# Attention and convolution-row matmuls in 64x64 tiles, row weights loaded pair by pair, and separate tiles for the second projection's weights and tokens

## The chip, the cores and the metric

The kernel runs on one core of one Trainium2 chip. Its time is the device time of one execution in microseconds; "before" is the median of three executions. The engines are called as the profile calls them: PE (TensorE matmul), PEld (its weight loads), DVE (VectorE), ACT (ScalarE), POOL (GpSimd) and SP (SyncE, which here does nothing but issue DMAs).

## The reference

Two layers work on x of shape (4, 512, 128, 64), in float32. B is 4, T is 512, and a token has D = 128 x 64 = 8192 channels.

```python
# layer 0, x as (b, t, d)
xn = layernorm(x);  k, v = xn @ Wk, xn @ Wv;  r = sigmoid(xn @ Wr)      # d -> 64
s_t = decay * s_(t-1) + k_t * v_t                                       # scan over t
x = x + (r * states) @ Wo                                               # 64 -> d: "attend"
x = x + gelu(conv3(layernorm(x)) + freq_b)                              # 64 -> 64 channels, along f
x = x + layernorm(depthwise_causal_conv3(layernorm(x)) + time_b)        # along t
x = x + gelu(x @ W1 + b1) @ W2 + b2                                     # 64 -> 256 -> 64
# layer 1
trend = moving_average(x, 25);  xf = rfft(x - trend)[:128 modes]
x = trend + irfft(xf mixed by complex weights of each channel)
```

## The kernel before

Layer 0 holds a batch's x with channels on the 128 partitions: 64 chunks of 128 channels by 512 tokens, taken as NPR = 32 pairs of chunks. For each batch b these stages run, named by letters in the code:

- J `project`: k, v and r for all pairs, accumulated in one PSUM pair of banks (L414). Each pair needs its projection weights, x with channels on partitions (`xp`, 512 KB), and x with tokens on partitions (512 KB), of which DVE takes the layernorm statistics (`bn_stats`, L346). The first batch also accumulates sums of the weights (L406).
- Z `scan`: a serial chain of small steps on PE, DVE, ACT and POOL that ends in `rst`, the gated states, and in the mean and deviation of the next layernorm.
- A `attend_and_convolve`: step i does `attend(i)`, `convolve(i - 2)` and the sums of pair i - 3 (`add_up`, L253). `attend` loads `xp` (L296) and `wo_sb` (L532), multiplies (L536), and DVE adds xp (L538) and scales (L542). `convolve` writes one pair of PSUM banks in three groups: the rows (L557: a product over two rows that carries the layernorm's mean and the constant term, four matmuls), the neighbours (L566: the convolution's reach across the chunks' edges, four 64x64 matmuls) and the chunk itself (L571: two 128x128 matmuls). ACT applies gelu (L572), DVE adds (L574), POOL's queue stores, ACT squares (L579).
- C `convolve_time`, O `open_feed`, F `feed_forward` (L743 widens and L758 narrows, both in 64x64 tiles; L779 transposes back to tokens).

"64x64 tiles" means that a matmul uses a quarter of PE's array: the partitions of its operands select the row half, the partitions of its output the column half, and four of them can run side by side. Before, attention uses two tiles of 64 rows by 128 columns, and the rows use four of 32 rows by 64 columns, for which `cgr` keeps the rows' weights of all 32 pairs at partitions 0, 32, 64 and 96. They are loaded once, by four DMAs on ACT's queue (L212).

PE's order is written out by hand (`manual_schedule`). `in_turn` runs two streams side by side and picks at each yield the one that is behind:

```python
((0, (Z, 0.12), (A, 0.88)), (1, (J, 0.88), (Z, 0.12))),      # A0 beside J1
((0, (C, 1.0)), (1, (A, 1.0))),                              # C0 beside A1
((0, (O, 0.05), (F, 0.95)), (2, (J, 0.88), (Z, 0.12))),      # F0 beside J2
((1, (C, 1.0)), (2, (A, 1.0))),                              # C1 beside A2
```

and so on. `project(0)` comes before all of it. On the other engines a scheduler orders the instructions when the program is built; each engine and each DMA queue then runs its list strictly in that order, and waits on semaphores.

Tiles come from pools with a fixed number of buffers. `fr` has the front stages' tiles (`xp`, `x1`, `z`, `wo`, `wcs`, `cgr`), `wxp` has two buffers of the tag `wx`. In J1, one `wx` buffer holds a pair's projection weights and its tokens together (L394), but for the first nine pairs, which borrow `x1` and `z`. In J2 and J3 a `wx` buffer holds the weights of two pairs (L354). In the last two feed-forwards it holds a pair of finished chunks (L766). Layer 1's pools `dft`, `slabs` and `io` reuse the storage from its start, in this order.

Of the kernel before, what the change touches and what calls it, by code (L numbers as in the profile page):

```python
# [10 lines left out]
F32 = mybir.dt.float32  # L11
# [5 lines left out]
P = 128  # L17
T = 512
NF = 128
H = 64  # L20
# [60 lines left out]
def layer0(ctx, tc, dram, x, xt, vecs, wkvr, wo, wdec, wconv, fbias, w1, fb1, w2, fb2, x4):  # L81
# [54 lines left out]
    fb2_sb = load("fb2_sb", fb2)  # L136


    sel = const.tile([P, 2, 2, S], F32, name="sel")
    for k in range(2):  # L140
        for i in range(2):
            nc.vector.tensor_copy(sel[:, k, i, :], ident[:, k * S : (k + 1) * S])
# [5 lines left out]
    nc.vector.tensor_copy(decb, dec.to_broadcast([P, T]))  # L148


    cgr = fr.tile([P, NPR, H], F32, name="cgr", bufs=1)

    at_one = const.tile([P, 2], F32, name="at_one")
    nc.vector.tensor_reduce(at_one[:, 0:1], ident.rearrange("p (q k) -> p q k", k=32)[:, :, 1], mybir.AxisListType.X, ALU.add)
# [15 lines left out]
    def prepare():  # L170
# [34 lines left out]
        nc.vector.tensor_copy(cgt, pg[:, 0, 0:P])  # L205
        for k in range(2):
            nc.scalar.dma_start(cgd[:, k, :], cgt[k * NCH : (k + 1) * NCH, :])
        cg4 = cgd.rearrange("(i j) k (h m) -> h j k i m", j=2, h=2)
        for h in range(2):
            for j in range(2):  # L210
                q = 32 * (2 * h + j)
                nc.scalar.dma_start(cgr[q : q + 2, :, :], cg4[h, j])  # L212

# [83 lines left out]
        return xp  # L297

    def spare(tag, n):
        if tag == "wx":  # L300
            return wxp.tile([P, 2, n], F32, tag=tag, name=tag)
        return fr.tile([P, 2, n], F32, tag=tag, name=tag, bufs=4 if tag == "z" else 3)

    def c_bank():
# [25 lines left out]
    def project(b):  # L330
# [20 lines left out]
        def weights(i):  # L351

            if i < NPR:
                w = spare("wx", 4 * S + SL).rearrange("p k n -> p (k n)")[:, 0 : 16 * S]  # L354
                w = w.rearrange("p (c s) -> p c s", c=4)
                nc.sync.dma_start(w, wkvr[2 * i : 2 * i + 4, :, 0 : 4 * S].rearrange("c p s -> p c s"))
                for k in range(2):
                    ws[i + k] = w[:, 2 * k : 2 * k + 2, :]
# [15 lines left out]
        for i in range(NPR):  # L374
            first, last = i == 0, i == NPR - 1
            if b > 1:


                xks[i] = token_major(i, two(bk, "sq" if i % 2 else "x2"))
                if i % 2 == 0:  # L380
                    weights(i + 2)
                if not last:
                    xps[i + 1] = load_x(b, i + 1)
                wq, xp = ws.pop(i), xps.pop(i)
                for k in (i - 2, NPR - 2, NPR - 1) if last else (i - 2,):
                    if k in xks:
                        statistics(k, xks.pop(k))
            else:
                if unscanned[0]:

                    wq, xk = two(fr, "x1")[:, :, 0 : 4 * S + 3], spare("z", SL)
                else:

                    both = spare("wx", 4 * S + SL)  # L394
                    wq, xk = both[:, :, 0 : 4 * S], both[:, :, 4 * S :]
                n = 4 * S + 2 * (b == 0)
                nc.sync.dma_start(wq[:, :, 0 : n], wkvr[2 * i : 2 * i + 2, :, 0 : n].rearrange("c p s -> p c s"))
                xp = load_x(b, i)
                statistics(i, token_major(i, xk))
            if b == 0:  # L400
                nc.gpsimd.memset(wq[:, :, n:], 1.0)
                for j in range(2):
# [24 lines left out]
    def scan(b):  # L427
# [43 lines left out]
        if b == 0:  # L471
            kv = two(fr, "x1")
        else:
            kv = spare("wx", 4 * S + SL)[:, :, 0:SL]
        for k in range(2):
            pk = bank()
            nc.tensor.matmul(
# [44 lines left out]
    def attend_and_convolve(b):  # L522
# [6 lines left out]
        def attend(i):  # L529
            xp = load_x(b, i)  # L530
            wo_sb = fr.tile([P, P], F32, tag="wo", name="wo_sb")
            nc.sync.dma_start(wo_sb, wo[:, i, :])  # L532
            at = two(ps_a, "a")
            for j in range(2):
                js = slice(j * S, (j + 1) * S)
                nc.tensor.matmul(at[:, j, :], lhsT=wo_sb[js, :], rhs=rst[js, :], start=True, stop=True)  # L536
            x1 = x1s[i] = fr.tile([P, 2, SL], F32, tag="x1", name="x1")
            nc.vector.tensor_tensor(x1, at, xp, ALU.add)  # L538
            z = fr.tile([P, 2, SL], F32, tag="z", name="z", bufs=4)
            for j in range(2):  # L540
                zs[2 * i + j] = z[:, j, :]
            nc.vector.tensor_tensor(z, x1, pair_of(rb), ALU.mult)  # L542

        def scaled(i):

            wcs = fr.tile([P, 2, P + H], F32, tag="wcs", name="wcs")
            for j in range(2):
                c = 2 * i + j
                ws[c] = wcs[:, j, :]
                nc.scalar.mul(wcs[:, j, :], wc_sb[:, i % 2, :], vec[:, G2, c : c + 1])  # L550

        def convolve(i):
            cv = c_bank() if i % 2 or held[0] else two(ps_m, "m")
            for h in range(2):
                for j in range(2):
                    q = 32 * (2 * h + j)
                    nc.tensor.matmul(  # L557
                        cv[h * H : (h + 1) * H, j, :], lhsT=cgr[q : q + 2, i, :], rhs=mb[q : q + 2, :],
                        start=True, stop=False,
                    )  # L560
            for j in range(2):
                c = 2 * i + j
# [162 lines left out]
    def feed_forward(b):  # L725
# [26 lines left out]
        def narrow(i, q):  # L752
# [10 lines left out]
                return  # L763
            x3 = x3s.pop(i)
            if lag > 1:
                pair = spare("wx", 4 * S + SL)[:, :, 0:SL]  # L766
# [130 lines left out]
def layer1(ctx, tc, x4, wri, dftv, dftd, dfte, idfte, idfto, avg, avgh, out, after):  # L897
# [67 lines left out]
    def transform(b, xf):  # L965

        for g in range(NS // 2):
            edge = slabs.tile([P, SL], F32, tag="edge", name="edge")
            uv, ev, pf = [], [], []
            for k in range(2):  # L970
                s = 2 * g + k
# [82 lines left out]
    def invert(b, xf):  # L1054
# [24 lines left out]
        def trends(s):  # L1079
            c = slice(s * SL, (s + 1) * SL)  # L1080
            xin = slab(b, s)
            halo = slabs.tile([P, SL], F32, tag="edge", name="halo")
            for j in range(NT):
                at = 32 * j
                if j > 0:
# [137 lines left out]
```

## Time and profile before

| | us |
|---|---|
| median of three executions (3697.53 to 3706.25) | 3703.95 |
| the profiled execution | 3708.95 |
| its span | 3707.2 |
| PE busy | 3520.8 (95%) |
| DVE busy | 2669.1 (72%) |
| ACT busy | 1778.5 (48%) |
| J0, then `scan(0)` | 0 to 166, to 225 |
| A0 beside J1 and its scan | 225 to 544 |
| C0 beside A1 | 544 to 815 |
| F0 beside J2 | 815 to 1205 |
| C1 beside A2 | 1205 to 1460 |
| F1 beside J3 | 1460 to 1862 |
| C2 beside A3 | 1862 to 2115 |
| F2 beside C3, then F3 | 2115 to 2480, to 2742 |
| layer 1 | 2742 to 3707 |

A line of the profile names the source line, the engine, the operation, the output and input tiles (buffer numbers left out), PE's tile shape where there is one, and the shapes; then how many, their busy time, and the mean duration of one in ns. A float32 matmul appears as two records, so x8 in the timeline are four matmuls. Times of the stages are read from the starts of their lines in the trace; neighbouring stages overlap a little.

### The profile page before, as it was taken

Reading aid. Unit: us, or ns where it says so; the run is one execution under the profiler, and the core shown is the slowest. Engines: PE = TensorE matmul, PEld = TensorE weight load, DVE = VectorE, ACT = ScalarE, POOL = GpSimd, SP = SyncE. Lnnn points to the kernel's source line nnn. Section 1 sums busy time; section 2 is a strip of 40 time slices with the busy share of each in tenths; the row PEclk is TensorE's granted clock in tenths of the full one; section 3 lists DMA queues with packets and bytes.
Section 4 is the critical chain, followed back from the end, with each engine's and each line's share of the span. In section 5 each row is a group of like instructions: output and inputs, shape, how many; then the busy total and the mean of one; then the engine's idle time right before and its main releaser. Section 6 shows DMA issues by size and latency. Waiting matters only on the chain. (4 is left out here: it accounts for less than half of the span.)

```text
span 3707.2 us, 52993 instructions
## 1 busy us (share of the span) xinstructions
PE 3520.8 (95%) x20041; PEld 1358.2 (37%) x20041; DVE 2669.1 (72%) x3498; ACT 1778.5 (48%) x2331; POOL 449.0 (12%) x654
## 2 busy tenths in 40 slices
PE   9999999989999999999999989999999999999998
PEld 4433322224433223433322333333333833328433
DVE  4445559986777896677789799956668277892677
ACT  0013336656666565666656588878864200152100
POOL 0000012220111121011112121100000000001000
PEclk9999989999999999999999999999999999999999
DMA  9857747777885687888568677746658478994687
GB/s 305 282 197 246 238 144 261 260 268 270 289 291 190 234 280 267 275 292 291 180 225 285 228 240 257 237 176 216 223 184 279 150 246 292 298 297 164 215 285 262
DMA packets 427223, 910.29 MB, mean 246 GB/s; under 512 B 32728, under 2 KB 83160, under 8 KB 422872
## 3 DMA queue, kind: packets, MB, share of 16 engines
q1 hardware_dynamic: 353136, 636.92, 52.6%
q0 software_dynamic: 71680, 268.46, 20.1%
q8 instruction: 160, 2.62, 0.3%
q10 hardware_dynamic: 2152, 1.51, 0.1%
q14 instruction: 95, 0.78, 0.1%
HBM read 638.26 MB, written 268.50 MB: 245 GB/s over the span
## 5 line engine op out<-in xcount | busy, mean ns | idle before, releaser
L758 PE MATMUL p<-mid,w_sb 64*64 64x512 f32 x2048 | 553.1, 597 | 17.5 <-DVE wx L771 17.5
L758 PE MATMUL pb<-mid,w_sb 64*64 64x512 f32 x2048 | 535.3, 597 | 0.0
L748 ACT ACTIVATE mid<-m,fb_sb 128x1024 f32<-128x1024 f32 x256 | 284.9, 1113 | 92.2 <-PE m L743 90.9
L748 ACT ACTIVATE mid<-c,fb_sb 128x1024 f32<-128x1024 f32 x256 | 284.5, 1111 | 92.2 <-PE c L743 90.0
L743 PE MATMUL c<-x,w_sb 64*64 64x512 f32 x2016 | 280.6, 609 | 13.9 <-ACT mid L748 7.6
L743 PE MATMUL m<-x,w_sb 64*64 64x512 f32 x2016 | 282.6, 612 | 7.4 <-ACT ob L792 5.3
L758 PEld LDWEIGHTS p<-mid,w_sb 64*64 64x64 f32 x2048 | 154.0, 135 | 292.4 <-issue 262.7
L1069 ACT COPY two<-a 128x512 f32<-128x512 f32 x64 | 37.5, 586 | 430.1 <-PE a L1064 430.1
L414 PE MATMUL a<-xp,wx 128*128 128x512 f32 x512 | 237.4, 608 | 0.5 <-DVE me L270 0.5
L1092 PE MATMUL b<-xin,avg_sb 128*128 128x512 f32 x512 | 230.8, 593 | 3.3 <-DVE xin L1098 3.3
L1098 DVE TENSOR_TENSOR xin<-b,pm 128x512 f32<-128x512 f32 x256 | 159.0, 683 | 98.7 <-PE b L1095 83.7
L579 ACT ACTIVATE sq<-x 128x1024 f32<-128x1024 f32 x128 | 135.1, 1055 | 184.0 <-DVE x L574 184.0
L634 DVE SCALAR_TENSOR_TENSOR to<-kd,vec,to 128x510 f32<-128x510 f32 (+1 forms) x272 | 196.8, 742 | 9.3 <-ACT to L630 8.2
L711 ACT ACTIVATE kd<-kd,vec 128x512 f32<-128x512 f32 x256 | 192.7, 803 | 3.3 <-DVE kd L703 3.3
L253 PE MATMUL st<-x,ones 128*32 128x512 f32 x512 | 175.6, 610 | 14.0 <-DVE x L574 14.0
L944 DVE COPY xf<-b 128x256 f32<-128x256 f32 x128 | 54.4, 425 | 178.9 <-PE b L1038 170.0
L714 DVE TENSOR_TENSOR x<-kd,kx 128x1024 f32<-128x1024 f32 x126 | 154.1, 1223 | 36.2 <-ACT kd L711 36.2
L634 DVE SCALAR_TENSOR_TENSOR z<-x,vec,z 128x511 f32<-128x511 f32 x240 | 175.8, 745 | 5.0 <-ACT z L630 3.6
L538 DVE TENSOR_TENSOR x<-a,xp 128x1024 f32<-128x1024 f32 x128 | 156.0, 1219 | 30.9 <-PE a L536 28.6
L536 PE MATMUL a<-rst,wo_sb 64*128 64x512 f32 x512 | 149.8, 659 | 26.2 <-DVE x L538 24.2
L577 POOL DMA_DIRECT2D x<-x x128 | 93.6, 731 | 569.7 <-DVE x L574 564.7
L771 DVE SCALAR_TENSOR_TENSOR x4t<-p,fb_sb,x 128x512 f32<-128x512 f32 x64 | 47.8, 746 | 159.5 <-PE pb L758 157.1
(269 smaller groups left out, 6823.4 us busy)
## 6 DMA issues: line engine op xcount, KB each, us to landing
xp<-in_xt SPq DMA_DIRECT2D x256, 512.0 KB
kh<-to SPq DMA_DIRECT2D x156, 512.0 KB
x<-x POOLq DMA_DIRECT2D x128, 512.0 KB, 4.6
kx<-x SPq DMA_DIRECT2D x128, 512.0 KB
x<-ob POOLq DMA_DIRECT2D x64, 1024.0 KB, 8.1
xin<-x SPq DMA_DIRECT2D x64, 1024.0 KB
out<-xin POOLq DMA_DIRECT2D x64, 1024.0 KB, 6.4
x<-x SPq DMA_DIRECT2D x96, 512.0 KB
```

The costliest lines, as they stand in the source:

```text
L253: nc.tensor.matmul(st[32 * q : 32 * q + 32, :], lhsT=ones, rhs=src[:, j, :], start=first, stop=last,)
L414: nc.tensor.matmul(pa[:, k, :], lhsT=wq[:, j, k * P : (k + 1) * P], rhs=xp[:, j, :], start=first and j == 0, stop=last and j == 1,)
L536: nc.tensor.matmul(at[:, j, :], lhsT=wo_sb[js, :], rhs=rst[js, :], start=True, stop=True)
L538: nc.vector.tensor_tensor(x1, at, xp, ALU.add)
L634: tap = nc.vector.scalar_tensor_tensor(to[:, j, k:], xr[:, j, : SL - k], vec[:, w, c], to[:, j, k:], ALU.mult, ALU.add)
L711: tc.keep_in_program_order(nc.scalar.activation(d[:, j, :], d[:, j, :], AF.Identity, bias=vec[:, B4, c], scale=vec[:, G4, c]))
L714: nc.vector.tensor_tensor(x3, d, x2, ALU.add)
L743: nc.tensor.matmul(pm[halves[j], h, :], lhsT=w1_sb[halves[h], q * H : (q + 1) * H], rhs=x3[halves[h], j, :], start=True, stop=True,)
L748: gelu = nc.scalar.activation(mid, pm, AF.Gelu_apprx_tanh, bias=fb1_sb[:, q : q + 1])
L758: nc.tensor.matmul(sums2[i][j][halves[h], :], lhsT=w2_sb[halves[j], q, :], rhs=mid[halves[j], h, :], start=q == 0, stop=q == 3,)
L1092: nc.tensor.matmul(po[j], lhsT=avg_sb[:, j, :], rhs=xin[:, j, :], start=True, stop=False)
L1098: nc.vector.tensor_tensor(by_n(xin[:, j, :]), by_n(po[j]), by_c(pm[j % 2][:, j // 2, :]), ALU.add)
```

## The change

- `attend` makes four matmuls of 64x64 out of two of 64x128.
- `convolve` makes the rows' matmuls over 64 partitions instead of two, in four 64x64 tiles. Their weights stand in three tiles `cg0`, `cg1` and `cg2` of 128x128 that are zero but for two rows in each half; `scaled(i)` loads these two rows for each chunk of pair i by two DMAs of 1 KB on SP's queue, into tile i % 3. `cgr` and its four DMAs go. (The rows of `mb` that meet zeros are any rows of it.)
- The neighbours' code is as it was.
- In J1, weights have a tag of their own, `wk` with two buffers, and tokens take `wx`, now 4 KB instead of 6 KB a partition, with three buffers. J1's statistics of a pair are written after the next pair's loads.
- The other users of `wx` have three buffers of it too. `sel` moves from `const` to `fr`; layer 1's `edge` and `halo` move from `slabs` to `io`, with as many buffers as before.

```diff
-    sel = const.tile([P, 2, 2, S], F32, name="sel")
+    sel = fr.tile([P, 2, 2, S], F32, name="sel", bufs=1)
...
-    cgr = fr.tile([P, NPR, H], F32, name="cgr", bufs=1)
+    cgs = [fr.tile([P, P], F32, name=f"cg{k}", bufs=1) for k in range(3)]
+    for cg in cgs:
+        nc.gpsimd.memset(cg, 0.0)
...
-        cg4 = cgd.rearrange("(i j) k (h m) -> h j k i m", j=2, h=2)
-        for h in range(2):
-            for j in range(2):
-                q = 32 * (2 * h + j)
-                nc.scalar.dma_start(cgr[q : q + 2, :, :], cg4[h, j])
...
-        if tag == "wx":
-            return wxp.tile([P, 2, n], F32, tag=tag, name=tag)
+        if tag in ("wk", "wx"):
+            return wxp.tile([P, 2, n], F32, tag=tag, name=tag, bufs=2 if tag == "wk" else 3)
...
-                    both = spare("wx", 4 * S + SL)
-                    wq, xk = both[:, :, 0 : 4 * S], both[:, :, 4 * S :]
+                    wq, xk = spare("wk", 4 * S), spare("wx", SL)
...
-                statistics(i, token_major(i, xk))
+                xks[i] = token_major(i, xk)
+                for k in (i - b, NPR - 1) if last else (i - b,):
+                    if k in xks:
+                        statistics(k, xks.pop(k))
...
             for j in range(2):
-                js = slice(j * S, (j + 1) * S)
-                nc.tensor.matmul(at[:, j, :], lhsT=wo_sb[js, :], rhs=rst[js, :], start=True, stop=True)
+                for hs in halves:
+                    nc.tensor.matmul(
+                        at[hs, j, :], lhsT=wo_sb[halves[j], hs], rhs=rst[halves[j], :], start=True, stop=True
+                    )
...
         def scaled(i):
+            for j in range(2):
+                at = H * (j ^ i % 2)
+                nc.sync.dma_start(cgs[i % 3][at : at + 2, :], cgd[2 * i + j])
...
-            for h in range(2):
-                for j in range(2):
-                    q = 32 * (2 * h + j)
+            for j in range(2):
+                rs = halves[j ^ i % 2]
+                for hs in halves:
                     nc.tensor.matmul(
-                        cv[h * H : (h + 1) * H, j, :], lhsT=cgr[q : q + 2, i, :], rhs=mb[q : q + 2, :],
-                        start=True, stop=False,
+                        cv[hs, j, :], lhsT=cgs[i % 3][rs, hs], rhs=mb[rs, :], start=True, stop=False
                     )
...
-            edge = slabs.tile([P, SL], F32, tag="edge", name="edge")
+            edge = io.tile([P, SL], F32, tag="edge", name="edge")
```

More of the change, by code (lines that the diff above doesn't have):

```diff
@@ L353, in weights @@
             if i < NPR:
-                w = spare("wx", 4 * S + SL).rearrange("p k n -> p (k n)")[:, 0 : 16 * S]
-                w = w.rearrange("p (c s) -> p c s", c=4)
+                w = spare("wx", SL).rearrange("p k n -> p (k n)").rearrange("p (c s) -> p c s", c=4)
                 nc.sync.dma_start(w, wkvr[2 * i : 2 * i + 4, :, 0 : 4 * S].rearrange("c p s -> p c s"))
@@ L473, in scan @@
         else:
-            kv = spare("wx", 4 * S + SL)[:, :, 0:SL]
+            kv = spare("wx", SL)
         for k in range(2):
@@ L765, in narrow @@
             if lag > 1:
-                pair = spare("wx", 4 * S + SL)[:, :, 0:SL]
+                pair = spare("wx", SL)
                 x4s[i] = [pair[:, j, :] for j in range(2)]
@@ L1081, in trends @@
             xin = slab(b, s)
-            halo = slabs.tile([P, SL], F32, tag="edge", name="halo")
+            halo = io.tile([P, SL], F32, tag="edge", name="halo")
             for j in range(NT):
```

## The prediction

> **What bounds the kernel now.** I read the page first, then busy time by stage, then the matmuls in order of time at one place of the attention stage and at one of the feed-forward, then the waits of the first attention stage. TensorE is the bound of the whole:
>
> ```profile
> span 3707.2 us, 52993 instructions
> ...
> PE 3520.8 (95%) x20041; PEld 1358.2 (37%) x20041; DVE 2669.1 (72%) x3498; ACT 1778.5 (48%) x2331; POOL 449.0 (12%) x654
> ...
> DVE  4445559986777896677789799956668277892677
> ```
>
> DVE reaches 9 in some slices, so stages must be told apart. These four stretches hold all of `attend_and_convolve`: A0 beside J1, A1 beside C0, A2 beside C1, A3 beside C2 (columns: length, then busy time of PE, PEld, DVE, ACT, POOL, granted clock, DMA share, GB/s). The last two rows cut the second stretch, and the chain that ends `scan(0)`.
>
> ```profile
> 225.00:544.00 319.00, 307.99 (x1335) 95.65 (x1335) 178.07 (x218) 104.42 (x146) 27.70 (x38) 0.97 0.66 220
> 544.00:815.00 271.00, 246.33 (x1231) 62.01 (x1233) 258.62 (x294) 160.93 (x219) 73.96 (x98) 0.98 0.76 261
> 1205.00:1460.00 255.00, 242.31 (x1372) 64.07 (x1364) 214.08 (x221) 152.66 (x207) 49.20 (x71) 0.99 0.75 256
> 1862.00:2115.00 253.00, 240.92 (x1324) 64.83 (x1320) 209.20 (x215) 146.30 (x197) 51.16 (x73) 0.97 0.73 249
> ...
> 700.00:750.00 50.00, 44.50 (x236) 10.53 (x228) 49.93 (x56) 31.48 (x43) 14.21 (x18) 1.00 0.76 256
> ...
> 186.00:228.00 42.00, 34.00 (x108) 16.18 (x108) 12.47 (x30) 5.63 (x7) 1.27 (x2) 0.96 0.35 117
> ```
>
> PE is busy 97%, 95% and 95% of stretches 1, 3 and 4. Stretch 2 belongs to DVE: 258.62 of 271, and in its middle 49.93 of 50. In `scan(0)` every queue has room.
>
> Now PE in order of time: first a pair of A1 (stretch 2), then the feed-forward, whose matmuls are 64x64 tiles already. The first column is the start; what a group costs is the distance to the next group's start, since ends overlap.
>
> ```profile
> 711.93 1.13 PE L536 MATMUL a<-rst,wo_sb 64*128 64x512 f32 x4
> 712.99 1.09 PE L557 MATMUL m<-rm,cgr 2*64 2x512 f32 x8
> 714.00 1.09 PE L566 MATMUL m<-z,wcs 64*64 64x512 f32 x8
> 715.02 1.98 PE L571 MATMUL m<-z,wcs 128*128 128x512 f32 x4
> ...
> 1005.64 1.09 PE L743 MATMUL m<-x,w_sb 64*64 64x512 f32 x8
> 1006.55 0.59 PE L758 MATMUL p<-mid,w_sb 64*64 64x512 f32 x2
> ...
> 1007.41 1.04 PE L743 MATMUL c<-x,w_sb 64*64 64x512 f32 x8
> ...
> 1011.70 0.59 PE L758 MATMUL p<-mid,w_sb 64*64 64x512 f32 x2
> ...
> 1012.67 0.70 PE L414 MATMUL a<-xp,wx 128*128 128x512 f32 x1
> ```
>
> A group of four 64x64 matmuls costs 0.86 (1006.55 to 1007.41) between neighbours of its own shape, 0.91 (1005.64 to 1006.55) just after another shape, 0.97 (1011.70 to 1012.67) just before another. Change of shape on both sides is then 0.86 + 0.05 + 0.11 = 1.02, which is what the rows (L557, 32x64 tiles: 1.01) and the neighbours (L566: 1.02) take. Attention (L536, two 64x128 tiles) takes 1.06.
>
> **The change part by part.**
>
> *Attention, rows and neighbours in one shape.* Where attention stands just before the rows, the three groups take 1.06 + 1.01 + 1.02 = 3.09 now; in one shape they take 0.91 + 0.86 + 0.97 = 2.74: 0.35 less. In the built order of PE, which the change does not alter otherwise, that is so for 106 of the 128 pairs (24, 26, 28 and 28 of the four batches). In the other 22, attention alone gains 1.06 - 1.02 = 0.04, rows with neighbours 2.03 - 1.88 = 0.15. Sum of PE: 106 x 0.35 + 22 x 0.19 = 41 us, some 10 to 10.6 in each stretch.
>
> Two rules of the Trainium skill bear on this. "TensorEngine Tiling (Array Packing)", Key Properties, says that a change of tiling mode drains the array; the trace puts 0.16 on each, which is the gain above. Its Gotcha 1 says that different row tiles cannot use one PSUM bank at a time. Today's rows write each bank from two row tiles, so by the rule they would run as two rounds, 2 x 0.86, and the new mapping (one row tile for each bank) would save another 0.86 x 128 = 110 us. The row is 1.01, one round; nothing is taken for it.
>
> What arrives on the end: stretch 1, PE-bound, all 10. Stretch 2: nothing, since PE only waits more for DVE, which has the same work. Stretches 3 and 4: PE idles some 12 of 255, of which about 7 for DVE (L538 and L574), and a faster PE meets DVE (84% busy) more often; I take 9 of 10.6 in each. Together 10 + 0 + 9 + 9 = 28.
>
> *Rows' weights loaded pair by pair.* Four early DMAs go from ACT's queue; 256 DMAs of 1 KB come onto SP's, two a pair, and three memsets on POOL before anything waits. "DMA: Bandwidth & Descriptors", Rules for kernel authors, speaks against this: under 64 KB one pays mostly overhead, with a fixed cost of about 2 us. Were it exposed, 256 x 2 = 512 us. The nearest rows are SP's issues of `wo_sb`, 0.42 to 0.53 us each. Two more make 0.9 us in a step of about 8.5 us (SP issues `xp` at 703.3 and 711.9), where SP now issues three and mostly waits. The wait that they add is for the rows three pairs earlier (L557); queued behind it on SP are `xp` and `wo_sb` of two pairs on. In the built order they stand between `wo_sb` and `xp` of pair i+2, and that `xp` waits for L538 of pair i-1 anyway, which falls in the step of that same L557. Landing has two steps, 17 us. So nothing, bounds 0 to 0.9 x 128 = 115 us if SP were the bound; nearest to 0, since no PE row waits for `xp` or `wo_sb` now.
>
> *J1's tokens and weights apart, statistics a pair later.* Now both share a buffer of two, so a token load waits for PE's matmuls. Apart, the tokens wait for DVE's statistics alone, and the built order pulls them far forward: 3 more of J1's token loads stand before J0's last pair on SP, and between DVE's first constants of `scan(0)` (186) and A0's first addition (L538, 228) come the statistics of 16 pairs, where none stood.
> - J0: 3 x 0.52 MB at its 300 GB/s is 5 us, if DMA is what ends it; 0, if PE is (busy 10.0 of 10 from 140 to 150). I take 3.
> - `scan(0)`: 16 pairs x 1.29 us of statistics = 21 us of DVE, which has 42 - 12.5 = 29 free; 8.4 MB beside the 4.9 moved there (117 GB/s x 42) is 13.3, at 300 GB/s 44 us of 42. Both just fit. But DVE takes them in order, and an instruction of the chain stands behind a statistic that waits for its landing or runs 0.65 us: I count some eight such places, 5 us. Bounds 0 and 53 (the third rival).
> - A0 beside J1: 19 statistics pairs and their waits leave DVE:
>
> ```profile
> DVE stt L346 <- DMA wx<-in_x: 40.5, 20, 4.2
> DVE wx L363 <- DMA wx<-in_wkvr: 40.0, 18, 4.5
> ```
>
> But PE, not DVE, is the bound there; of its 11 us idle only 3.9 are for L538. I take 1 of gain (0 to 4).
>
> *Storage.* `sel`, and `edge` and `halo` in another pool, cost no instruction. The first `edge` copies of layer 1 now stand behind the last copies of layer 0 on ACT (end 2743.1); three by 0.63 end at 2745, and PE takes them up at 2748.6. Third `wx` buffers in J2, J3 and the last feed-forwards: PE idles there for L771, not for a buffer. Nothing, 0 to 3 either way.
>
> Sum: -28 + 3 + 5 - 1 = -21 us. The profiled execution took 3708.95 (span 3707.2, 1.75 around it), 5.0 above the median of the runs, 3703.95. On that median: 3683.
>
> **The rivals.**
> 1. All of it arrives: DVE keeps up in stretches 3 and 4, tokens fit into the scan for nothing, A0 gains 4: -10 - 10.6 - 10.6 - 4 = -35, 3669; 0.15. For it: DVE has 16% free there. Against: L538 and L574 already hold PE.
> 2. The gain ends at DVE in stretches 3 and 4 as in stretch 2: -10 + 8 - 1 = -3, and 3701; 0.13. For it: the waits named. Against: PE is 95% busy, DVE 84%.
> 3. Slower: the token loads hold up `scan(0)`. A load and its statistics in turn cost 2.0 (the 40.5 over 20 waits above) + 1.29 = 3.3; 16 in turn are 53 us, if none runs beside the chain's own waits. With J0's 5, against 29 gained: +29, 3733. It decides from 29 us on; 0.1. For it: one in-order queue, every statistic waits for a DMA. Against: three buffers keep three loads in flight, and 29 of the 42 us are free.
>
> **How the numbers follow.** The forecast (-21) has 0.62. A difference under 0.2%, 7.4 us, is about what a measurement of this kernel can tell from none. Faster: 0.62 + 0.15, less a little where J0 and the scan cost more: 0.76. Same: rival 2, 0.13. Slower: 0.11. The range reaches up to 3705, where rival 2 and a scan that costs 25 lie, and down to 3661, past rival 1 by its 8 us in stretch 2.
>
> **What would show it.** PE after: L536 to L557 0.91, L557 to L566 0.86, L566 to L571 0.97; PE's total some 41 us less. Stretch 2 as long as before, stretches 3 and 4 about 246 and 244, A0 beside J1 about 308. L538 of A0's first pair near 236 instead of 228. I am wrong if the three groups stay near 3.09, if PE waits for L557's weights, or if A0 starts after 257.

## The result and the profile after

The changed kernel takes 3686.77 us (median of 7 executions, 3673.13 to 3694.55); the kernel before, on the same chip, 3699.18 (7 executions, 3692.01 to 3706.25). The ratio is 0.9967, with a 95% interval of 0.9954 to 0.9979: 12 us less, between 8 and 17. The profiled executions differ by more, 3708.95 against 3685.27. The page of the changed kernel, with the lines that answer to those of before, and two groups of matmuls; then the same two groups in the kernel before:

```profile
span 3683.5 us, 54528 instructions
...
PE 3480.4 (94%) x20553; PEld 1372.7 (37%) x20553; DVE 2671.6 (73%) x3498; ACT 1778.1 (48%) x2331; POOL 448.4 (12%) x657
...
DVE  4464469986777896677789799956677277892677
...
L250 PE MATMUL st<-x,ones 128*32 128x512 f32 x512 | 183.9, 609 | 23.8 <-DVE x L576 23.7
...
L534 PE MATMUL a<-rst,wo_sb 64*64 64x512 f32 x1024 | 143.3, 630 | 27.4 <-DVE x L538 25.3
```

```profile
L253 PE MATMUL st<-x,ones 128*32 128x512 f32 x512 | 175.6, 610 | 14.0 <-DVE x L574 14.0
...
L536 PE MATMUL a<-rst,wo_sb 64*128 64x512 f32 x512 | 149.8, 659 | 26.2 <-DVE x L538 24.2
```

PE's busy total fell by 40 us, and the end by 24 in these two executions: PE waits more. The sums of a pair (L250, L253 before) waited 14.0 us for the residual (L574 before, L576 now), and now 23.8. Five stretches by busy time (length, PE, PEld, DVE, ACT, POOL, granted clock, DMA share, GB/s), first of the kernel before, then of the changed one. They are cut at the same instructions in both, and closer than the prediction's stretches:

```profile
186.00:229.00 43.00, 34.00 (x108) 16.18 (x108) 13.47 (x31) 5.63 (x7) 1.27 (x2) 0.96 0.35 116
229.00:545.00 316.00, 307.47 (x1338) 96.21 (x1338) 176.39 (x216) 104.58 (x146) 27.70 (x38) 0.97 0.66 220
545.00:808.00 263.00, 238.61 (x1198) 58.72 (x1198) 256.29 (x287) 159.09 (x218) 71.95 (x95) 0.98 0.76 258
...
1226.00:1457.00 231.00, 222.46 (x1243) 58.42 (x1246) 203.86 (x212) 142.35 (x196) 48.47 (x70) 0.99 0.80 270
...
1876.00:2114.00 238.00, 229.38 (x1256) 61.43 (x1257) 201.62 (x209) 141.30 (x192) 50.71 (x72) 0.97 0.76 259
```

```profile
189.00:238.00 49.00, 38.19 (x116) 17.57 (x120) 32.75 (x61) 5.63 (x7) 1.27 (x2) 0.86 0.80 264
238.00:538.00 300.00, 290.94 (x1482) 98.06 (x1474) 157.29 (x184) 104.71 (x146) 27.68 (x38) 0.98 0.61 205
538.00:801.00 263.00, 232.41 (x1306) 62.67 (x1306) 256.68 (x286) 158.81 (x218) 70.90 (x95) 0.99 0.77 257
...
1219.00:1448.00 229.00, 216.13 (x1358) 62.70 (x1362) 203.82 (x212) 142.24 (x196) 48.36 (x70) 0.99 0.81 272
...
1865.00:2098.00 233.00, 221.73 (x1378) 66.13 (x1378) 202.52 (x210) 141.42 (x193) 50.83 (x72) 0.99 0.78 265
```

They are `scan(0)`, A0 beside J1, C0 beside A1, C1 beside A2 and C2 beside A3. DVE is at 256.68 of 263 in the third (256.29 before). And PE in order of time at one pair of A2 of the changed kernel:

```profile
1306.42 1.09 PE L534 MATMUL a<-rst,wo_sb 64*64 64x512 f32 x8
1307.33 1.04 PE L560 MATMUL m<-rm,cg 64*64 64x512 f32 x8
1308.19 1.04 PE L568 MATMUL m<-z,wcs 64*64 64x512 f32 x8
1309.15 0.70 PE L573 MATMUL m<-z,wcs 128*128 128x512 f32 x1
```

From start to start these are 0.91, 0.86 and 0.96 us; 0.91, 0.86 and 0.97 were forecast. Over all pairs at full clock and without a wait, the medians are 0.91, 0.86 and 0.97 (101, 124 and 118 groups), and 1.06, 1.02 and 1.02 before.

For all comparisons between kernels I cut the profiled execution at the same DVE instructions (the end of the first constant of `scan(0)`, of the first L538, of the two copies that follow the sums of a batch, and of the first and the last residual of a stage). The first number is the length; the second is the time in which PE's granted clock was 0.5, times one half, that is what full clock would have saved if PE were the bound all through. The clock drops to one half for 3.4 us or a multiple of it, 30 times before and 24 times after, and these windows differ between executions; so a difference of 3 us in one stage can be nothing else. "Corrected" below means length less that second number; where PE isn't the bound, as in `scan(0)`, it takes off too much.

PE's 40 us hold such windows too: the halves of those in which PE was busy sum to 62 us before and 45 after, so 17 of the 40 are clock.

| us | before | after | tiles alone | tokens alone | statistics in order | cg twice | cg twice, own tiles |
|---|---|---|---|---|---|---|---|
| J0 | 186.0, 5.1 | 189.1, 3.4 | 188.8, 3.4 | 182.6, 5.1 | 186.6, 1.7 | 188.3, 3.4 | 188.8, 3.4 |
| scan(0) | 43.0, 1.7 | 48.4, 6.8 | 43.4, 1.7 | 62.8, 13.7 | 43.6, 1.8 | 49.3, 5.1 | 48.4, 5.1 |
| A0/J1 | 316.2, 10.2 | 300.4, 5.1 | 302.3, 5.1 | 312.0, 8.5 | 301.7, 5.0 | 310.3, 10.2 | 305.3, 1.7 |
| C0/A1 | 263.0, 5.1 | 263.3, 3.4 | 265.0, 5.5 | 263.5, 6.8 | 263.4, 3.4 | 265.1, 5.1 | 263.8, 3.4 |
| C1/A2 | 230.8, 3.4 | 229.0, 3.4 | 232.2, 5.1 | 229.9, 1.7 | 229.0, 1.7 | 238.9, 6.8 | 230.3, 5.1 |
| C2/A3 | 238.9, 6.8 | 233.1, 3.4 | 234.1, 3.4 | 237.1, 3.4 | 233.5, 3.4 | 243.6, 6.8 | 233.2, 3.4 |
| layer 1 | 965.8, 8.2 | 963.3, 5.2 | 975.5, 11.2 | 967.3, 5.1 | 970.4, 8.8 | 968.6, 6.1 | 968.9, 8.1 |
| whole span | 3707.2, 68.0 | 3683.5, 54.7 | 3702.1, 60.7 | 3717.7, 70.0 | 3684.7, 49.7 | 3722.3, 69.3 | 3694.9, 54.1 |

Of the 23.7 us between the two profiled executions, up to 13.3 are fewer half-clock windows; what is left, 10.4, fits the medians' 12. The gain is made in A0/J1 (-15.8, corrected -10.7). It is lost in C0/A1 (+0.3), and mostly in C1/A2 (-1.8) and C2/A3 (-5.8, corrected -2.4). Layer 1, which none of the first runs alters in its work, lies between 963 and 976: that is how far an unaltered stage can be off.

### The profile page after: what moved, and what is told of

It is laid out like the page before. It is cut to its first block, busy times and chain, and to the rows that moved or that the text cites. A ratio compares the mean times of both kernels' runs of the same rounds, so it can differ in the third digit from the quotient of the medians.

```text
span 3683.5 us, 54528 instructions
## 1 busy us (share of the span) xinstructions
PE 3480.4 (94%) x20553; PEld 1372.7 (37%) x20553; DVE 2671.6 (73%) x3498; ACT 1778.1 (48%) x2331; POOL 448.4 (12%) x657
## 5 line engine op out<-in xcount | busy, mean ns | idle before, releaser
L760 PE MATMUL p<-mid,w_sb 64*64 64x512 f32 x2048 | 549.3, 595 | 17.9 <-DVE wx L773 17.9
L1094 PE MATMUL b<-xin,avg_sb 128*128 128x512 f32 x512 | 230.8, 593 | 3.3 <-DVE xin L1100 3.3
L250 PE MATMUL st<-x,ones 128*32 128x512 f32 x512 | 183.9, 609 | 23.8 <-DVE x L576 23.7
L636 DVE SCALAR_TENSOR_TENSOR to<-kd,vec,to 128x511 f32<-128x511 f32 (+1 forms) x272 | 197.0, 743 | 11.5 <-ACT to L632 8.0
L538 DVE TENSOR_TENSOR x<-a,xp 128x1024 f32<-128x1024 f32 x128 | 156.1, 1219 | 48.1 <-PE a L534 45.5
L534 PE MATMUL a<-rst,wo_sb 64*64 64x512 f32 x1024 | 143.3, 630 | 27.4 <-DVE x L538 25.3
L773 DVE SCALAR_TENSOR_TENSOR x4t<-p,fb_sb,x 128x512 f32<-128x512 f32 x64 | 47.7, 746 | 160.0 <-PE pb L760 157.5
L704 DVE TENSOR_TENSOR kd<-kh,rm 128x1024 f32<-128x1024 f32 x128 | 155.6, 1219 | 6.8 <-ACT rm L284 4.6
```

The costliest lines, as they stand in the source:

```text
L250: nc.tensor.matmul(st[32 * q : 32 * q + 32, :], lhsT=ones, rhs=src[:, j, :], start=first, stop=last,)
L636: tap = nc.vector.scalar_tensor_tensor(to[:, j, k:], xr[:, j, : SL - k], vec[:, w, c], to[:, j, k:], ALU.mult, ALU.add)
L704: nc.vector.tensor_tensor(d, to, pair_of(rb), ALU.mult)
L760: nc.tensor.matmul(sums2[i][j][halves[h], :], lhsT=w2_sb[halves[j], q, :], rhs=mid[halves[j], h, :], start=q == 0, stop=q == 3,)
L1094: nc.tensor.matmul(po[j], lhsT=avg_sb[:, j, :], rhs=xin[:, j, :], start=True, stop=False)
```

## The experiments

Runs that were made together share a chip and the runs of the kernel before, and kernels are compared by their ratios to it. Edits are against the changed kernel unless said otherwise. In the texts on record, T is as a rule the prediction's own account; rivals are named where they stand.

**One part alone.** First the tiles with J1 left as it was (the other users of `wx` are back at two buffers too; those lines are left out):

```diff
-        if tag in ("wk", "wx"):
-            return wxp.tile([P, 2, n], F32, tag=tag, name=tag, bufs=2 if tag == "wk" else 3)
+        if tag == "wx":
+            return wxp.tile([P, 2, n], F32, tag=tag, name=tag)
...
-                    wq, xk = spare("wk", 4 * S), spare("wx", SL)
+                    both = spare("wx", 4 * S + SL)
+                    wq, xk = both[:, :, 0 : 4 * S], both[:, :, 4 * S :]
...
-                xks[i] = token_major(i, xk)
-                for k in (i - b, NPR - 1) if last else (i - b,):
-                    if k in xks:
-                        statistics(k, xks.pop(k))
+                statistics(i, token_major(i, xk))
...
```

> The changed kernel with J1 as before (weights and tokens of a pair in one of two buffers, statistics at once); attention and rows in 64x64 tiles and the 256 small DMAs stay. Theory T (gains come from PE's shape changes alone; in the stretches beside C they are handed back to DVE; J1's part only moves token loads into scan(0), where they cost): J0 and scan(0) as before (A0's first L538 near 229 instead of 237.6), A0 beside J1 about 306, the rest as in the changed kernel: about 17 us faster than before, 5 faster than the changed kernel. Rival 'tokens pay' (J1's part frees DVE in A0 and is what made that stretch 16 us shorter): A0 beside J1 stays at 313 or more, and the whole is 5 us faster than before at most. Rival 'small DMAs' (what is missing in the stretches beside C1 and C2 is lost on SP): no different from T here.

Measured: 3699.73 us, ratio 0.9982 (0.9972 to 0.9992). A0/J1 is 302.3, nearly that of the full change (corrected, 8.7 of its 10.7 us), so the shape of the tiles is what shortens it; J1's own part adds some 2 (the next run has 2.4 with it alone). `scan(0)` is 43.4. By the ratios this kernel is some 6 us behind the full change; why isn't settled. Its profile is longer by 12 us in layer 1 and by 5 in F0/J2, and 10.8 of these 17 are half-clock loss.

Then the kernel before with only J1's part (weights and tokens in tiles of their own, two buffers of each since `cgr` keeps its storage, and statistics a pair later):

```diff
-                    both = spare("wx", 4 * S + SL)
-                    wq, xk = both[:, :, 0 : 4 * S], both[:, :, 4 * S :]
+                    wq, xk = spare("wk", 4 * S), spare("wx", SL)
...
-                statistics(i, token_major(i, xk))
+                xks[i] = token_major(i, xk)
+                for k in (i - b, NPR - 1) if last else (i - b,):
+                    if k in xks:
+                        statistics(k, xks.pop(k))
...
```

> The kernel before with J1's part alone: weights and tokens in tiles of their own, statistics a pair later, two buffers of each, because three do not fit beside the old row weights; 18 pairs of statistics then stand in scan(0). Theory T: J0 and scan(0) together 5 to 9 us longer, A0 beside J1 0 to 3 shorter, the rest the same: 3 to 8 us slower than before. Rival 'tokens pay': A0 beside J1 at least 6 us shorter, the whole equal or up to 5 us faster.

Measured: 3722.30 us, ratio 1.0048 (1.0034 to 1.0062): slower by 17 us, more than twice what theory T allowed. The chain of `scan(0)` takes 62.8 instead of 43.0. Its waits there (engine, line, what it waited for; us, times, longest):

```profile
ACT rg L493 <- DVE rg L492: 31.8, 1, 31.8
...
DVE stt L346 <- DMA wx<-in_x: 16.1, 10, 4.2
```

DVE stands at ten statistics for token loads, 16.1 us in all, with the chain's next step queued behind them: ACT's sigmoid waits 31.8 us for DVE, where it waits 17.9 in the full change. This is the prediction's third rival in miniature: 36 statistics of J1 stand inside the chain, and some of their loads aren't there in time. In the full change, with three buffers and 32 statistics, the same line has 8 waits and 11.1 us. That the third buffer makes the difference is likely, but no run changed the buffers alone.

**The statistics kept in program order.** One edit:

```diff
-                if b > 1:
+                if b > 0:
                     tc.keep_in_program_order(stats)
```

> The changed kernel, in which J1's statistics keep their written place on DVE, so that 5 pairs of statistics instead of 16 stand in scan(0). Theory T: A0's first L538 near 230 instead of 237.6, A0 beside J1 306 to 308, the rest the same: 3 to 7 us faster than the changed kernel, about 17 faster than before. Rival 'tokens pay': A0 beside J1 grows by more than scan(0) gives back, and the whole is slower than the changed kernel by 3 us or more.

Measured: 3686.12 us, ratio 0.9950 (0.9934 to 0.9966). Ten statistics stand in the chain instead of 32, `scan(0)` is 43.6, and A0/J1 stays at 301.7. So hoisting the statistics brings next to nothing in A0/J1 (1.3 us), and `scan(0)` is 5 us shorter without it, though nearly all of these 5 may be half-clock windows (see the part on the prediction). It is the lowest ratio of any kernel here that leaves nothing out; its interval meets that of the full change.

**The small loads of the rows' weights.** Each is issued twice:

```diff
                 nc.sync.dma_start(cgs[i % 3][at : at + 2, :], cgd[2 * i + j])
+                nc.sync.dma_start(cgs[i % 3][at : at + 2, :], cgd[2 * i + j])
```

> The changed kernel with each of the 256 small DMAs of the rows' weights issued twice, 512 in all. Theory T (they cost nothing, DVE takes the gain): within 3 us of the changed kernel, stretches beside C1 and C2 unchanged. Rival 'small DMAs' (they hold up SP's queue and took 7 us in each of these two stretches): as much again, 10 to 20 us slower than the changed kernel, most of it beside C1 and C2.

Measured: 3712.51 us, ratio 1.0018 (1.0008 to 1.0027), 18 us behind the full change. By the text on record the rival has won. But the queue's own waits show something that the original loads don't have:

```profile
SPq L549 <- DMA cg<-cgd: 254.7, 148, 4.6
```

The second load writes the tile that the first is writing, so SP holds its whole queue 1.7 us until the first has landed. So the run was made again, with the second load going to tiles of its own that nobody reads:

```diff
+    spares = [fr.tile([P, P], F32, name=f"cs{k}", bufs=1) for k in range(3)]
...
                 nc.sync.dma_start(cgs[i % 3][at : at + 2, :], cgd[2 * i + j])
+                nc.sync.dma_start(spares[i % 3][at : at + 2, :], cgd[2 * i + j])
```

> The changed kernel with every small load of row weights issued a second time as before, but into three tiles of its own that nothing reads, so that the second load does not wait for the first to land. In the run with the load doubled into the same tile, SP waited 254.7 us in 148 second loads for the first ones. Theory W (the wait on SP cost the 18 us there; the loads themselves cost nothing): within 4 us of the changed kernel, the stretches A0/J1, C1/A2 and C2/A3 within 3 of it. Rival Q (256 more small loads cost by their issue on SP and their place in the queue): 10 to 20 slower, some 8 to 10 in each of these stretches, as in that run.

Measured: 3697.13 us, ratio 0.9992 (0.9980 to 1.0005), some 9 us behind the full change: between the two theories. The built order moved as well: 18 statistics of J1 stand in `scan(0)` instead of 32. By stage: C0/A1, C1/A2 and C2/A3 are within 1.3 us of the full change, where the run before lost 10 in each of the last two; there the wait was the cost and the loads are free. In A0/J1 the loads cost 4.9 (corrected 8); the moved statistics hardly explain it, since A0/J1 was 301.7 with ten of them in the scan. PE's waits for a load there, in this run and then in the full change:

```profile
PE m L413 <- DMA xp<-in_xt: 5.7, 4, 2.3
```

```profile
PE m L412 <- DMA xp<-in_xt: 1.0, 1, 1.0
```

In A0/J1 two stages load their pairs through SP at once, and J1's `xp` comes late when 64 more loads stand on the queue. Another 5.6 us of this profile (corrected 2.7) lie in layer 1, which has no such load.

The opposite test takes the small loads off SP, on top of the statistics in order:

```diff
-                nc.sync.dma_start(cgs[i % 3][at : at + 2, :], cgd[2 * i + j])
+                nc.gpsimd.dma_start(cgs[i % 3][at : at + 2, :], cgd[2 * i + j])
```

> The changed kernel with J1's statistics kept in program order (36 -> 10 before A0, as in the run with that one edit, 3686.1 us) and the 256 small loads of row weights issued from POOL's queue instead of SP's. Theory D: the loads cost nothing on SP, since SP waits for buffers most of the time; within 3 us of the run with the statistics alone, PE's idle time in the four stretches as there. Theory Q: SP's queue is free of them, 3 to 6 us less in each of the four stretches, 8 to 20 in all. The opposite is open too: a load behind POOL's store of a pair arrives too late and the row matmuls wait for it, 5 us and more.

(The text counts 36 statistics; that is the number of the tokens-alone run, the changed kernel has 32.) Measured: 3694.54 us, ratio 0.9986 (0.9972 to 0.9999). C0/A1 265.2, C1/A2 231.4, C2/A3 233.4: nothing is won where DVE has its peaks. A0/J1 is 310.3, 8.6 longer than with the loads on SP (3.5 of it half clock). Both theories missed: the kernel is slower than the one with the statistics in order, by 13 us by the ratios. POOL's queue is no better place for the loads. Why A0/J1 grew isn't settled. The third possibility on record, rows that wait for their weights, isn't it: the rows' matmuls (L560) wait there for the residual (L576, 6.6 us against 3.6), and none of them for a load.

**The start.** With the loads' tiles, PE's first projection in J0 starts at 11.81 us instead of 7.03. PE and DVE at the start, first of the full change:

```profile
9.20 1.29 DVE L343 BATCH_NORM_STATS2 stt<-z 128x6 f32<-128x512 f32 x2 [9.20 <-DMA z<-in_x]
...
11.44 0.32 DVE L359 TENSOR_SCALAR x<-x,vec 128x192 f32<-128x192 f32 x1
...
11.81 2.93 PE L412 MATMUL a<-xp,x 128*128 128x512 f32 x3 [4.88 <-DVE x L359]
```

The scheduler has put the first statistics ahead of the first scaling of weights, and they wait for a token load until 9.20. The three clearings of `cg0` to `cg2` stand on POOL ahead of the clearing of J0's weight columns; to test whether they tip the order, they were put behind it (on top of the statistics in order). The second view is of that kernel:

```diff
-    for cg in cgs:
-        nc.gpsimd.memset(cg, 0.0)
...
                 nc.gpsimd.memset(wq[:, :, n:], 1.0)
+                if 0 < i < 4:
+                    nc.gpsimd.memset(cgs[i - 1], 0.0)
```

> The changed kernel with J1's statistics kept in program order and the three clearings of the row-weight tiles moved on POOL behind the first ones of J0's weight columns. Theory M (the start of J0: the clearings delay the columns' own, so the first statistics stand ahead of the first weight scaling on DVE, which then waits for a token load): PE's first projection group starts near 7 instead of 11.3 us, J0 is 3 to 5 us shorter than in the run with the statistics alone, all else equal. Rival, the reason given in the prediction (three token loads of J1 ahead of J0's last pair): the start moves but J0 ends where it did, 0 in all, because the loads at its end decide.

```profile
5.89 0.32 DVE L357 TENSOR_SCALAR x<-x,vec 128x192 f32<-128x192 f32 x1 [5.89 <-PE psum_w L404]
...
7.09 4.81 PE L412 MATMUL a<-xp,x 128*128 128x512 f32 x8 [0.37 <-DVE x L357]
9.14 1.29 DVE L341 BATCH_NORM_STATS2 stt<-z 128x6 f32<-128x512 f32 x2 [2.06 <-DMA z<-in_x]
```

The scaling is first again and PE starts at 7.09; J0 is 180.8 instead of 186.6 (corrected 179.1 against 184.9). Theory M holds. All runs fall into two groups by this: J0 corrected is 181.7 to 185.7 in the eight kernels that start near 11.5 and 177.4 to 180.9 in the six that start near 7. J1's token loads ahead of J0's last pair, the rival's reason, moved along: 5 before, 8 in the changed kernel, 6 with the statistics in order, 4 here. But they do not decide. From 20 us to the end of J0, PE waits for no load itself in any of these four; it waits for DVE's scalings, 6.2 us before and less, 3.3, after:

```profile
PE a L414 <- DVE x L363: 6.2, 5, 2.2
```

```profile
PE a L412 <- DVE x L359: 3.3, 4, 1.3
```

And the kernel with the tiles alone has 8 such loads without J1's part; the one with J1's part alone has 5. On the whole the run took 3685.46 us, ratio 0.9964 (0.9950 to 0.9978); against 0.9950 without this edit, on another chip, the intervals don't resolve 4 us.

**Where the gain of C0/A1, C1/A2 and C2/A3 went.** The prediction took DVE's load in the last two from an average (84%). Cut into 30 us, C1/A2 of the kernel before reads:

```profile
1250.00:1280.00 30.00, 30.00 (x180) 7.90 (x172) 29.58 (x31) 18.92 (x27) 6.15 (x8) 1.00 0.87 295
1280.00:1310.00 30.00, 27.21 (x142) 7.01 (x140) 29.97 (x33) 17.77 (x24) 8.92 (x11) 1.00 0.85 289
1310.00:1340.00 30.00, 28.87 (x160) 7.55 (x160) 28.05 (x29) 19.77 (x27) 6.18 (x10) 1.00 0.84 276
1340.00:1370.00 30.00, 29.22 (x177) 7.80 (x176) 28.46 (x30) 19.75 (x27) 5.48 (x9) 1.00 0.82 287
1370.00:1400.00 30.00, 29.57 (x176) 7.56 (x168) 27.05 (x27) 17.34 (x25) 6.31 (x9) 1.00 0.81 269
1400.00:1430.00 30.00, 28.81 (x164) 7.38 (x160) 28.13 (x29) 21.32 (x30) 6.89 (x11) 1.00 0.79 275
```

DVE is busy 171 of these 180 us: 95%, with 99% and 100% in the first two. The 84% came with the 75 us around it, in which DVE has 43. PE is busy 174 of the same 180, 96%: the two engines are about equally full here, and what PE saves arrives only as far as DVE has room too. To see whether DVE takes the gain, both kernels were run with less DVE work: first without the subtraction of the means in the time convolution's norm.

```diff
-        nc.vector.tensor_tensor(xr, xr, pair_of(mb), ALU.subtract)
```

> The kernel before, with the second DVE instruction of the time convolution's norm left out (the subtraction of the row of means, 128 x 1024, 1.22 us each, 128 of them): the mean's subtraction is not computed. It frees some 21 to 30 us of DVE in each stretch in which a time convolution lies beside another batch's work. It is read against the next kernel, which is the changed kernel with the same instruction left out. Both theories expect it faster than the kernel before by its PE waits in these stretches that end at DVE: about 8 in each of the three stretches behind the first and up to 20 in the last of batch 3, 25 to 45 us together.

> The changed kernel with the same subtraction left out. Theory D (DVE took the gain of the 64x64 tiles in stretches 2 to 4): with DVE relieved the tiles' gain comes through, so this kernel's time minus that of the one before it in this call is about -10 in each of C0/A1, C1/A2 and C2/A3 where the full pair has 0, -2 and -6, and the two differ by 28 to 36 us in all. Theory Q (the 256 small loads of row weights on SP's queue took it): the pair differs as the full pair does, by 10 to 16, and the three stretches by 0, -2 and -6 again.

Measured: 3616.41 (ratio 0.9776, 0.9758 to 0.9794) and 3601.28 us (0.9737, 0.9719 to 0.9755). The first is 81 us faster than the kernel before, where 25 to 45 were expected: DVE held more than the waits that were counted. The pair differs by 15.1 us; theory D's number of 28 to 36 is missed. For C0/A1 its rows, in both kernels, show why:

```profile
534.00:765.00 231.00, 215.24 (x1199) 57.49 (x1200) 223.23 (x255) 158.58 (x217) 75.79 (x95) 0.99 0.87 294
```

```profile
534.00:766.00 232.00, 214.60 (x1307) 64.63 (x1308) 223.37 (x256) 158.68 (x218) 75.78 (x95) 0.98 0.87 294
```

The stretch lost 32 us for 33 us taken off DVE, one for one, and DVE is as full as before (97%): the relief was too small to hand the stretch to PE. C1/A2 is another matter:

```profile
1175.00:1398.00 223.00, 220.91 (x1244) 58.45 (x1246) 183.76 (x194) 142.34 (x196) 46.09 (x70) 0.98 0.81 280
```

```profile
1176.00:1395.00 219.00, 212.06 (x1362) 62.05 (x1362) 183.81 (x194) 141.79 (x196) 45.73 (x70) 0.98 0.83 285
```

Here the relief made PE the bound of the kernel before (99% busy, DVE 82%), and still only 4 of PE's 9 us arrive (corrected 2). So theory D's miss is explained for C0/A1 alone. To give DVE more room everywhere, the third tap was taken away as well:

```diff
-            for k, w in ((1, W1), (2, W0)):
+            for k, w in ((1, W1),):
```

> The kernel before, with the subtraction of the row of means and the third tap of the time convolution (two DVE instructions of 0.745 us a pair) left out: neither is computed. In C0/A1, where DVE was busy 256 of 263 us and the first relief of 33 us took 32 us off the stretch, 48 us more come off DVE. It is read against the next kernel. PE's waits in C0/A1 (16 us with the first relief) should fall below 8.

> The changed kernel with the same two parts left out. Theory D (where DVE is the bound the tiles give nothing, and they give their PE time as soon as PE is): against the kernel before with the same parts left out, C0/A1 is now 7 to 10 us shorter (it was equal in the full pair and with the first relief), C1/A2 and C2/A3 7 to 9 each, and the whole 25 to 35. Rival L (not DVE's load but the length of the chain from an attention pair's convolution over gelu, residual and square to its sums holds PE, whatever DVE's load): C0/A1 stays within 3 of equal, C1/A2 and C2/A3 gain 2 to 6 each, the whole 12 to 18.

Measured: 3591.95 (ratio 0.9708, 0.9686 to 0.9729) and 3565.78 us (0.9629, 0.9608 to 0.9650). The three stretches, kernel before with both left out, then the changed kernel:

```profile
530.00:739.00 209.00, 205.50 (x1198) 55.33 (x1198) 183.73 (x191) 160.29 (x218) 81.54 (x96) 1.00 0.93 322
1149.00:1377.00 228.00, 221.01 (x1242) 58.26 (x1246) 158.13 (x155) 144.31 (x196) 48.65 (x70) 0.96 0.79 274
1788.00:2017.00 229.00, 222.54 (x1258) 60.81 (x1259) 157.35 (x154) 142.35 (x192) 49.70 (x72) 0.97 0.78 269
```

```profile
540.00:741.00 201.00, 197.69 (x1306) 59.04 (x1306) 182.29 (x189) 160.53 (x218) 81.58 (x96) 0.99 0.95 335
1149.00:1367.00 218.00, 209.70 (x1362) 60.95 (x1362) 157.48 (x155) 142.72 (x196) 48.66 (x70) 0.98 0.83 287
1774.00:1993.00 219.00, 211.36 (x1372) 63.39 (x1373) 156.41 (x153) 141.61 (x192) 49.70 (x72) 0.98 0.82 282
```

In the kernel before, PE is now busy 98% of the first stretch and DVE 88%, and the tiles' gain comes through:

| after less before, us | full pair | first relief | second relief |
|---|---|---|---|
| C0/A1 (corrected) | +0.3 (+2.0) | +0.8 (-0.9) | -7.7 (-9.4) |
| C1/A2 (corrected) | -1.8 (-1.8) | -3.9 (-2.2) | -9.8 (-4.7) |
| C2/A3 (corrected) | -5.8 (-2.4) | -5.5 (-5.5) | -9.4 (-6.0) |
| medians | -12.4 | -15.1 | -26.2 |

For C0/A1 this is plain: DVE's load took the gain. Rival L, which wanted that stretch equal whatever DVE's load, falls. For the other two the direction is the same and the gain grows, but half of the 9.8 and a third of the 9.4 are half-clock windows of the kernel before; 5 to 6 of the 9 that PE saves is what these runs show. Since C1/A2 gave up so little with the first relief, it is not shown that DVE's load took all of the gain in these two.

**A version with POOL.** On top of the statistics in order and the later clearings, POOL subtracts the means for every second pair that isn't pinned:

```diff
-        nc.vector.tensor_tensor(xr, xr, pair_of(mb), ALU.subtract)
+        engine = nc.gpsimd if i % 2 and not pinned else nc.vector
+        engine.tensor_tensor(xr, xr, pair_of(mb), ALU.subtract)
```

> A version that might beat both: the changed kernel with J1's statistics in program order and the clearings later, and with the subtraction of the means in the time convolution put on POOL instead of DVE for every second pair outside the pinned ones (nothing left out). Theory D: DVE loses 1.22 us in 16 pairs of C0/A1, 20 us in all, and that stretch 12 to 18 us if POOL takes under 4 us for one and does not slow DVE; 15 to 35 in all stretches. Against it: POOL may take so long for one, or hold up its stores of pairs behind it, that the taps come late: then slower by 5 to 40.

Measured: 3697.43 us, ratio 0.9990 (0.9978 to 1.0002), some 10 us behind the kernel without it by the ratios; C0/A1 is 276.3, 13 longer (corrected 8). From the page, then from the order of time:

```profile
L628 POOL TENSOR_TENSOR kd<-kd,rm 128x1024 f32<-128x1024 f32 x30 | 74.3, 2475 | 18.0 <-DVE kd L624 11.0 <-ACT rm L282 5.5
```

```profile
1929.71 1.22 DVE L624 TENSOR_TENSOR kd<-x,rm 128x1024 f32<-128x1024 f32 x1
1930.84 0.74 DVE L637 SCALAR_TENSOR_TENSOR to<-kd,vec,to 128x510 f32<-128x510 f32 x1
...
1931.00 2.81 POOL L628 TENSOR_TENSOR kd<-kd,rm 128x1024 f32<-128x1024 f32 x1
1931.62 3.28 DVE L624 TENSOR_TENSOR kd<-x,rm 128x1024 f32<-128x1024 f32 x1
```

POOL needs 2.5 us where DVE needs 1.22, and DVE's next multiplication (L624), issued 0.6 us after POOL's start, takes 3.28 instead of 1.22: it ends at 1934.90, 1.08 after POOL's end. Every long one of its kind ends 1.08 us behind POOL, every long tap 0.55: they do their work only when POOL is done. So DVE isn't relieved. 46 fewer DVE instructions save 56 us by their own durations, and DVE's total fell by 4 (2670.0 to 2665.7). The Trainium skill, "SBUF — State Buffer", Who interferes with whom, has this: a DVE instruction with two inputs in SBUF contends with a GpSimd one that reads SBUF, through a shared port that is an exclusive lock, and one with at most one SBUF input does not. The trace agrees on both: of L624, L628 and L637, 28 of the 36 that lie beside a POOL subtraction are stretched and seven of the other eight had begun before it (POOL's then takes 2.8 to 3.4 us), while L538 and L576, which read PSUM and SBUF, keep 1.22 us in all 31 that lie beside it.

## Why the prediction was right or wrong

The forecast was -21 us; the medians show -12.4, and the corrected profiles -10.4. That the measured 3686.77 lies only 4 us from the forecast's 3683 is luck: the median of the kernel before came down by 5 us with more executions. The direction and the main mechanism were right; one term was too large, and two were right in size by luck, for a reason that isn't the one given. Corrected, the four stretches with attention gave 13 us of the 28, and J0 with `scan(0)` took 5 of the 8.

- *Attention, rows and neighbours: 41 us of PE.* Right. The three groups cost what the feed-forward's own rows said. Summed from start to start, attention and rows (L534 and L560) take some 8 us less in C0/A1, 9 in C1/A2, 10 in C2/A3 and 11 in A0/J1, where 10 to 10.6 were forecast for them and the neighbours. That PE's busy total fell by 40 as well is in part luck, since 17 of it are clock.
- *A0/J1: 10 arrives, 1 more from DVE.* Right: 10.7 corrected, of which the tiles alone give 8.7.
- *C0/A1: nothing arrives.* Right, and the mechanism is shown: with 33 us less on DVE the stretch is 32 shorter and the tiles still give nothing; they give when DVE falls to 88%.
- *C1/A2 and C2/A3: 9 of 10.6 arrives in each.* This step failed. "PE is 95% busy, DVE 84%" compared two averages over a stretch whose two ends are quiet on DVE. In its working part, read in C1/A2, DVE was at 95% and PE at 96%, so a faster PE soon waits for DVE: 2 arrive in each, corrected, which is near the second rival's nothing. With DVE relieved twice 5 to 6 arrive; what holds the rest, and why one relief brought so little in C1/A2, stays open. PE's saving of 9 in C1/A2 comes back as longer waits behind L566's, L571's and L253's groups (+2.5, +1.9, +2.7 from start to start), the last of them the sums that wait for the residual.
- *J0: +3.* Right in size (+3.1, corrected +4.8) by luck, wrong in cause. Not the three token loads: the tokens alone make J0 shorter, PE itself waits for no load there after the start, and moving the three clearings brings it back. The prediction put the clearings "before anything waits"; they take 0.2 us each and nothing in the trace waits for them, but with them in front the scheduler built another order on DVE. Why it did isn't shown.
- *scan(0): +5.* Right in size (+5.4) in this execution, and keeping the statistics in order takes it back (43.6). The working, eight places of 0.65 us on DVE, isn't shown: PE's idle time in this stretch grew by 1.6 only, and up to 5.1 of the 5.4 are more half-clock windows. Two other kernels with statistics in order had such windows too and took 45.8 and 47.7, so what the hoisting costs by itself is between 1 and 5.
- *Small loads on SP: nothing.* Right for three stretches. In A0/J1, 64 more of them cost 5 to 8; so the 64 that are there may cost a few us as well. No run took them away without something else. (The Trainium skill has the fixed cost of about 2 us in "DMA: Bandwidth & Descriptors" under Latency and other measured facts, not under the rules. The 1.7 us for which a second load stood behind the first one agree with it.)
- *The slower rival.* It did not come with three buffers. With two it did, at +20 us in `scan(0)`, less than its 53.

## What to carry to other kernels

Read the busy share of the second engine in windows of a few steps, not over the stage: here averages of 95% and 84% hid 96% and 95%, and a gain on the first engine passes only where the second has room. To learn whether an engine takes a gain, relieve it by enough that it stops being the bound, and compare both kernels; too small a relief looks like a refutation, as in C0/A1. When a new tile is cleared or loaded "before anything waits", look at what the order of the built program does to the first instructions of the neighbours.

## What the runs showed of the hardware

- PE's granted clock falls to 0.5 for 3.4 us or a multiple, 30 times in the kernel before and 24 times in the changed one, though PE is busy 94 to 95%. Half of the time in these windows, 39 to 70 us in the 14 profiled executions, is more than the effect of this change, and it was up to 13.3 of the 23.7 us between the two profiles. What sets a window off isn't shown.
- SP's queue stands still behind a load that has to wait: a second load into a tile, which this program makes wait until the first has landed, held all behind it for 1.7 us each, 254.7 us over 148 of them.
- A subtraction moved from DVE to POOL took twice as long (2.475 us against 1.22) and held up DVE's instructions with two SBUF inputs until it was done: a tap of 0.745 us had a median of 1.95 beside it (21 of them).
- Four float32 matmuls in 64x64 tiles (512 columns) cost 0.86 us from start to start between groups of their own shape, and 0.16 more between two other shapes (0.05 just after a change, 0.11 just before one).
